# An LSTM step on one core of Trainium2: the output gate's products last, tanh of c transposed in place of h, and the bias copied into standing banks

## The chip, the core and the metric

The kernel runs on one core of a Trainium2 chip. Its engines are TensorE (PE, with its weight loads shown apart as PEld), VectorE (DVE), ScalarE (ACT), GpSimd (POOL) and SyncE (SP), which here only issues transfers. The metric is the device time of one execution in microseconds (us), less is better; the median over the runs is what is compared.

## The reference, cut to what matters

The program is a chain of two layers, each a graph layer and a feed-forward part. The second part of the first layer is an LSTM that runs over the first axis of the normalised input: 64 sequences are the batch and 256 positions are the steps, with 256 hidden units. Every step needs the h of the step before.

```python
def step(carry, xp):                       # xp: x @ W_ih.T + b_ih + b_hh
    h, c = carry
    gates = xp + h @ W_hh.T                # 64 x 1024
    i, f, g, o = jnp.split(gates, 4, axis=-1)
    c = jax.nn.sigmoid(f) * c + jax.nn.sigmoid(i) * jnp.tanh(g)
    h = jax.nn.sigmoid(o) * jnp.tanh(c)
    return ((h, c), h)
...
logits = jnp.einsum('bth,lh->btl', lstm_out, W_lin) + b_lin
g = jax.lax.stop_gradient(jnp.argmax(logits, axis=-1).astype(lstm_out.dtype))[..., None]
w = g * lstm_out
inc = jnp.cumsum(w, axis=1)
prefix = inc - w
suffix = inc[:, -1:, :] - inc
return 2.0 * lstm_out + prefix * fw_att + suffix * bw_att
```

## The kernel before, in words

The kernel goes through its stages one after the other: the first graph layer with its weights' preparation, the LSTM (lines 626 to 809), the second graph layer, and the second feed-forward part. The change is in the LSTM stage alone. All arithmetic there is in float32.

**Layout.** The 256 hidden units are split in two halves j of 128 units. A tile of 128 partitions holds half j=0 of the 64 sequences on partitions 0 to 63 and half j=1 on partitions 64 to 127, with 128 units along the free axis, so c, h and each gate are 128x128. The four gates of a step stand side by side in one bank of PSUM, 512 columns in the order i, f, g, o. The normalised input lies transposed in XT, and `hT` (128 units by 2 halves by 64 sequences) is h transposed: both serve as the 64-column weights of a product, while `w_ih` and `w_hh` stream past.

**A step's gates.** A bank is opened by one bfloat16 product (`open_gates`, L667) that writes the bias, given as three bfloat16 parts for each half. Then come four products with `w_ih` (`project`) and four with `w_hh`, all through `add_to_gates` (L673): K=2 parts of the contraction times two halves j, each half in its own 64 columns of the TensorE array (`tile_position`). The profile shows two rows of PE for each float32 product, so eight rows for each group of four. Banks come from a pool of four separate tiles; the bias is written three steps ahead and the input products run two steps ahead.

**The order of a step.** TensorE: the four `w_hh` products of step t, the four `w_ih` products of step t+2, the logits of step t-1 (L689, two products with a 256x2 weight), the bias row of step t+3, and the transpose of h (L798). `tc.issue_after` ties each of these behind the one before it; what remains of the order on every engine is the scheduler's. ScalarE: sigmoid of i and f (`sg`, L780), tanh of g (`gt`, L781), sigmoid of o (`so`, L789), tanh of c (`th`, L791). VectorE: f times c (L786), i times g (L787), their sum (L788), h = so times th (L795), and after TensorE's transpose into PSUM the copy to `hT` (L800).

**The sums.** Every four steps (TS) `summed` takes the four h of a buffer: VectorE adds b_lin and compares the two logits to a mask g on 64 partitions (L722, L723), a transfer copies g to the other 64 partitions (L726), and then VectorE forms w = h g, its running sums, and the result x1 + 2 h + prefix fb - w bw, which SP stores. It is a generator: a part of it is put behind the copy to `hT` of each following step.

Beside the LSTM's first steps, VectorE works on the parameters of the last stage (L812 to L1003), which need nothing of the LSTM; the scheduler places this work between the steps.

Of the kernel before, what the change touches and what calls it, by code (L numbers as in the profile page):

```python
# [143 lines left out]
def kernel(ctx: ExitStack, tc: tile.TileContext, a: dict, out: bass.AP):  # L144
# [482 lines left out]
    with (  # L627
# [7 lines left out]
        tc.tile_pool(name="ps_g2", bufs=4, space=PSUM) as ps_g,  # L635
        tc.tile_pool(name="ps_h2", bufs=1, space=PSUM) as ps_h,
        tc.tile_pool(name="ps_l2", bufs=2, space=PSUM) as ps_l,
# [4 lines left out]
        w_lin = wp.tile([P, K, 2], F32, name="w_lin")  # L642
        b_lin = wp.tile([B, 2], F32, name="b_lin")
        nc.sync.dma_start(w_ih, a["W_ihT"].rearrange("(k p) g -> p k g", p=P))
        nc.sync.dma_start(w_hh, a["W_hhT"].rearrange("(k p) g -> p k g", p=P))
        nc.sync.dma_start(w_lin, a["W_lin"])
        nc.sync.dma_start(b_lin, a["b_lin"].partition_broadcast(B))
# [16 lines left out]
        def open_gates(t):  # L664

            pg = ps_g.tile([P, 4 * P], F32, name=f"pg2_{t}", tag="pg2")
            return pg, nc.tensor.matmul(pg, halves, bias6, start=True, stop=False)  # L667

        def add_to_gates(pg, by, w, last):

            for k in range(K):
                for j in range(2):
                    ins = nc.tensor.matmul(  # L673
                        half(pg, j),
                        by(k),
                        gates_of(w, k, j),
                        start=False,
                        stop=(last and k == K - 1),
                        tile_position=(0, j * B),
                    )  # L680
            return ins

        def project(t, pg):

            return add_to_gates(pg, lambda k: XT[:, k, t, :], w_ih, t == 0)

        def logits(pl, t, hT):
            for k in range(K):
                nc.tensor.matmul(  # L689
                    pl[:, t % TS, :],  # L690
                    hT[:, k, :],
                    w_lin[:, k, :],
                    start=(k == 0),
                    stop=(k == K - 1),
                )
# [17 lines left out]
        def summed(t, h, pl):  # L713
# [4 lines left out]
            if t + 2 * TS < N:  # L718
                x1_of.append(x1_steps(t + 2 * TS))
            l0 = y2.tile([B, TS], F32, name=f"l0_{t}", tag="l0")  # L720
            g = y2.tile([P, TS], F32, name=f"g_{t}", tag="g")
            nc.vector.tensor_scalar(l0, pl[:, :, 0], b_lin[:, 0:1], None, ALU.add)  # L722
            nc.vector.scalar_tensor_tensor(  # L723
                g[:B, :], pl[:, :, 1], b_lin[:, 1:2], l0, ALU.add, ALU.is_gt
            )
            nc.sync.dma_start(g[B:, :], g[:B, :])  # L726
            nc.vector.scalar_tensor_tensor(x1, h, 2.0, x1, ALU.mult, ALU.add)
            yield
            w = q2.tile([P, TS, P], F32, name=f"w_{t}", tag="w")
            nc.vector.tensor_tensor(w, h, over_units(g), ALU.mult)  # L730
            yield
# [5 lines left out]
            for i in range(1, TS):  # L737
                nc.vector.tensor_tensor(pre[:, i, :], pre[:, i - 1, :], w[:, i - 1, :], ALU.add)
            total = y2.tile([P, P], F32, name=f"total_{t}", tag="total")
            nc.vector.tensor_tensor(total, pre[:, TS - 1, :], w[:, TS - 1, :], ALU.add)  # L740
            nc.vector.tensor_tensor(pre, pre, over_steps(fb), ALU.mult)
            yield
            nc.vector.tensor_tensor(w, w, over_steps(bw), ALU.mult)
            nc.vector.tensor_tensor(x1, x1, pre, ALU.add)
            nc.vector.tensor_tensor(x1, x1, w, ALU.subtract)
# [3 lines left out]
            yield  # L749

        ahead = [open_gates(t)[0] for t in range(3)]
        for t in range(2):
            last_ins = project(t, ahead[t])
        c_prev = hT = h_buf = total = None
        parts = iter(())
        x1_of = [x1_steps(0), x1_steps(TS)]
        for t in range(N):
            pg = ahead.pop(0)  # L760
            if t > 0:
                last_ins = add_to_gates(pg, lambda k: hT[:, k, :], w_hh, True)
            if t + 2 < N:
# [41 lines left out]
        for _ in summed(N - TS, h_buf, pl):  # L805
            pass
# [972 lines left out]
```

## Time and profile before

| what | before |
|---|---|
| median of 17 runs | 4962.22 us (4940.71 to 4976.26) |
| the profiled execution's own time | 4955.38 us |
| its span | 4953.6 us |
| busy: PE, DVE, ACT, POOL | 87%, 78%, 45%, 40% of the span |
| LSTM stage | 645 to 1930 us of the span |

A row of the profile is an instruction or a group of them: line and engine, the operation, what it writes and reads by the program's names, the shape, and times. In a timeline, the first two numbers are the start and the length in us, and the bracket at the end tells how long the engine had been idle and which instruction ended that. In a list of groups, the numbers after the bar are busy time in us and the mean of one in ns, then idle time ahead of them. Ends of TensorE's rows are modelled: rows overlap, so their lengths don't add up to time, and their starts tell the pace.

### The profile page before, as it was taken

To read this page: it belongs to the slowest core of one execution; us is meant where nothing else is said; L and a number is where in the kernel's file an instruction comes from. 1 tells how busy PE (TensorE), PEld (TensorE's weight loads), DVE (VectorE), ACT (ScalarE), POOL (GpSimd) and SP (SyncE) were. 2 spreads that over 40 slices of the span, in tenths; PEclk is the share of its full clock that TensorE was granted. 3 is DMA by queue.
4 is the path that set the end of the run, shared out by engine and by line. 5 is a ranking of instruction groups with operands and counts; after the bars stand their busy time and mean duration, and the time that the engine had idled before them with its cause. 6 is when DMAs were issued, how large, how long until landed. Compare 5 with 4: busy or idle time off the path is not lost. (4 is left out here: it accounts for less than half of the span.)

```text
span 4953.6 us, 59162 instructions
## 1 busy us (share of the span) xinstructions
PE 4300.8 (87%) x18365; PEld 2366.7 (48%) x18366; DVE 3867.3 (78%) x8648; ACT 2241.2 (45%) x4246; POOL 1994.2 (40%) x2505
## 2 busy tenths in 40 slices
PE   8999978999999996888882388989999998999998
PEld 5666633333333333666671144544455454444555
DVE  7888867555555555777788798998989998899994
ACT  3555521222222222555561255555655565555564
POOL 2222220000000002555550566666666666666661
PEclk9999989999999998999995689999999999999999
DMA  5222211211111113555541788888888888888892
GB/s 139 87 83 84 84 42 48 74 26 30 26 28 29 26 31 88 158 166 166 164 157 40 262 290 277 288 297 281 300 295 277 300 294 278 276 283 292 292 302 45
DMA packets 456279, 830.53 MB, mean 168 GB/s; under 512 B 51595, under 2 KB 309138, under 8 KB 455954
## 3 DMA queue, kind: packets, MB, share of 16 engines
q0 software_dynamic: 183184, 613.07, 37.3%
q1 hardware_dynamic: 270884, 210.42, 14.5%
q8 instruction: 148, 2.42, 0.2%
q10 hardware_dynamic: 1886, 3.16, 0.2%
q14 instruction: 177, 1.45, 0.1%
HBM read 700.45 MB, written 127.04 MB: 167 GB/s over the span
## 5 line engine op out<-in xcount | busy, mean ns | idle before, releaser
L1409 POOL DMA_INDIRECT row<-wT_d,num x1065 | 1052.2, 988 | 549.8 <-issue 253.5
L1433 DVE SCALAR_TENSOR_TENSOR top<-row,val,top 128x1024 f32<-128x1024 f32 x696 | 890.9, 1280 | 8.4 <-remote 3.5
L673 PE MATMUL pg<-w_hh,hT 128*64 128x512 f32 x2040 | 498.5, 610 | 91.5 <-DVE hT L800 91.0
L1521 PE MATMUL po<-w_d,fu 128*128 128x256 f32 x2048 | 564.6, 401 | 3.8 <-DVE fu L1502 2.4
L1441 PE MATMUL pc_cl<-xr,w_c 128*128 128x512 f32 x1024 | 506.8, 620 | 47.3 <-issue 39.1
L1441 PE MATMUL pc_gg<-xr,w_gt 128*128 128x512 f32 x1024 | 499.4, 612 | 33.0 <-ACT gg L1452 31.2
L1491 DVE SCALAR_TENSOR_TENSOR pv<-u,prm,pv 128x512 f32<-128x512 f32 x512 | 383.0, 748 | 173.4 <-PE pv L1478 99.2
L673 PE MATMUL pg<-w_ih,XT 128*64 128x512 f32 x2048 | 484.9, 595 | 2.9 <-issue 2.9
L1521 PEld LDWEIGHTS po<-w_d,fu 128*128 128x128 f32 x2048 | 376.0, 195 | 225.6 <-issue 182.5
L780 ACT ACTIVATE sg<-pg 128x256 f32<-128x256 f32 x256 | 98.1, 383 | 832.2 <-PE pg L673 826.0
L1054 POOL TENSOR_TENSOR adjT<-adjT,ident 128x128 f32<-128x128 f32 x128 | 60.9, 491 | 1009.2 <-DMA adjT<-in_adjT_dram 1008.9
L1484 ACT ACTIVATE u<-pa,prm 128x512 f32<-128x512 f32 x512 | 384.2, 777 | 168.7 <-remote 43.4
L1478 PE MATMUL pv<-cl,minus 128*128 128x512 f32 x512 | 278.7, 627 | 61.6 <-ACT pv L1473 44.0
L1452 ACT ACTIVATE gg<-pc_gg,prm 128x512 f32<-128x512 f32 x256 | 176.1, 689 | 315.9 <-PE pc_gg L1441 137.2
L1441 PEld LDWEIGHTS pc_cl<-xr,w_c 128*128 128x128 f32 x1024 | 196.8, 199 | 227.7 <-issue 208.5
L1441 PEld LDWEIGHTS pc_gg<-xr,w_gt 128*128 128x128 f32 x1024 | 193.0, 195 | 210.0 <-issue 165.1
L259 DVE TENSOR_SCALAR xn<-x,mv,rstd 128x256 f32<-128x256 f32 x512 | 200.9, 422 | 115.9 <-POOL rstd L252 110.7
L673 PEld LDWEIGHTS pg<-w_ih,XT 128*64 128x64 f32 x2048 | 148.2, 138 | 298.5 <-issue 298.5
L1534 POOL DMA_INDIRECT out_dram<-sum,perm x128 | 216.2, 1689 | 175.5 <-ACT sum L1531 123.8
L1452 ACT ACTIVATE cl<-pc_cl,prm 128x512 f32<-128x512 f32 x256 | 175.5, 688 | 244.8 <-PE pc_cl L1441 143.1
L786 DVE TENSOR_TENSOR cc<-sg,cc 128x128 f32<-128x128 f32 x255 | 74.5, 292 | 257.3 <-ACT sg L780 255.6
L673 PEld LDWEIGHTS pg<-w_hh,hT 128*64 128x64 f32 x2040 | 124.5, 137 | 288.5 <-issue 148.2
(407 smaller groups left out, 8324.2 us busy)
## 6 DMA issues: line engine op xcount, KB each, us to landing
adjT<-in_adjT_dram SPq DMA_DIRECT2D x128, 256.0 KB, 2.8
row<-wT_d,num POOLq DMA_INDIRECT x1065
x<-in_x_dram SPq DMA_DIRECT2D x64, 256.0 KB, 2.6
x_d<-x SPq DMA_DIRECT2D x64, 256.0 KB, 2.6
x1s<-x_d SPq DMA_DIRECT2D x128, 128.0 KB, 2.8
x_d<-x1s SPq DMA_DIRECT2D x128, 128.0 KB, 2.5
x<-x_d SPq DMA_DIRECT2D x64, 256.0 KB, 2.8
res_d<-x SPq DMA_DIRECT2D x64, 256.0 KB, 2.4
```

The source lines that it names most:

```text
L259: nc.vector.tensor_scalar(xn[:, c, :], x[:, c, :], mv[:, c, 0:1], rstd[:, c : c + 1], ALU.subtract, ALU.mult)
L673: ins = nc.tensor.matmul(half(pg, j), by(k), gates_of(w, k, j), start=False, stop=(last and k == K - 1), tile_position=(0, j * B),)
L780: nc.scalar.activation(sg, pg[:, : 2 * P], AF.Sigmoid)
L1409: return lambda: nc.gpsimd.indirect_dma_start(new(("row", g, q, r), [P, FF]), None, wT_d, bass.IndirectOffsetOnAxis(ap=tiles["num", g, q][ ...
L1433: nc.vector.scalar_tensor_tensor(now, tiles["row", g, q, r], v, was, ALU.add, ALU.max)
L1441: nc.tensor.matmul(pc, wgt[:, k, f * P : (f + 1) * P], tiles["xr", g][:, k, :], start=(k == 0), stop=(k == K - 1),)
L1452: nc.scalar.activation(new((n, g, f), [P, CH]), tiles["pc", g, n, f], AF.Gelu if n == "cl" else AF.Sigmoid, bias=ff.col["bc" if n == "cl" ...
L1478: return lambda: nc.tensor.matmul(tiles["pv", g, f], minus, tiles["cl", g, f], start=False, stop=True)
L1484: return lambda: nc.scalar.activation(new(("u", g, f, k), [P, CH]), tiles["pa", g, f], AF.Relu, bias=of, scale=sc)
L1491: nc.vector.scalar_tensor_tensor(pv, tiles["u", g, f, k], sg, pv, ALU.mult, ALU.add)
L1521: nc.tensor.matmul(tiles["po", g, h][:, c, :], tiles["fu", g, f][:, q * P : (q + 1) * P], ff.w_d[:, f, :], start=False, stop=last and c == ...
L1534: return lambda: nc.gpsimd.indirect_dma_start(out_rows, place(i, 1), tiles["sum", g, q // NC][:, q % NC, :], None, compute_op=ALU.add)
```

## The change

The four banks become one tile `gates` with four parts, made once. Each is opened once by the bias product before the loop; one of them is copied to `b_all` in SBUF, and in the loop ScalarE copies `b_all` into a bank again after its step has read it (L810 of the new file), so no bias product is left in the loop. The `w_hh` products are issued as four of 384 columns (i, f, g) and then four of 128 columns (o). Instead of h, TensorE transposes `so` (L798) and `th` (L805); ScalarE copies the first out of PSUM (`soT`), and VectorE multiplies it with the second straight into `hT` (L808); h itself is formed behind that. The four `w_ih` products of step t+2 are spread: two ahead of the transpose of `so`, one between the transposes, one behind. The logits are formed by GpSimd: h times each row of W_lin, added down to 16 columns, reduced by VectorE, and the two halves of units added by one product with a matrix `twin` for every four steps, which gives the mask on all 128 partitions and saves its transfer. GpSimd also multiplies w by bw. The weights of the logits are spread over partitions by six transfers ahead of the loop. The loop stands under `manual_schedule`: on TensorE, ScalarE and VectorE the loop's instructions keep the order of the program text.

```diff
--- before.py
+++ after.py
@@ -632,19 +632,28 @@
...
-        tc.tile_pool(name="ps_g2", bufs=4, space=PSUM) as ps_g,
+        tc.tile_pool(name="ps_g2", bufs=1, space=PSUM) as ps_g,
...
-        tc.tile_pool(name="ps_l2", bufs=2, space=PSUM) as ps_l,
+        tc.tile_pool(name="ps_l2", bufs=1, space=PSUM) as ps_l,
...
-        w_lin = wp.tile([P, K, 2], F32, name="w_lin")
-        b_lin = wp.tile([B, 2], F32, name="b_lin")
+        b_lin = wp.tile([P, 2], F32, name="b_lin")
         nc.sync.dma_start(w_ih, a["W_ihT"].rearrange("(k p) g -> p k g", p=P))
         nc.sync.dma_start(w_hh, a["W_hhT"].rearrange("(k p) g -> p k g", p=P))
-        nc.sync.dma_start(w_lin, a["W_lin"])
-        nc.sync.dma_start(b_lin, a["b_lin"].partition_broadcast(B))
+        nc.sync.dma_start(b_lin, a["b_lin"].partition_broadcast(P))
+        w_lin = wp.tile([P, 2, P], F32, name="w_lin")
+        lin_d = dram.tile([2, K, P], F32, name="lin_d")
+        for i in range(2):
+            nc.sync.dma_start(lin_d[i], a["W_lin"][:, :, i].rearrange("p k -> k p"))
+        for j in range(2):
+            for i in range(2):
+                nc.sync.dma_start(w_lin[j * B : (j + 1) * B, i, :], lin_d[i, j].partition_broadcast(B))
+        twin = wp.tile([P, P], F32, name="twin")
+        for j in range(2):
+            nc.vector.tensor_tensor(twin[:, j * B : (j + 1) * B], ident[:, :B], ident[:, B:], ALU.add)
...
@@ -661,38 +670,28 @@
...
-        def open_gates(t):
-            pg = ps_g.tile([P, 4 * P], F32, name=f"pg2_{t}", tag="pg2")
-            return pg, nc.tensor.matmul(pg, halves, bias6, start=True, stop=False)
-        def add_to_gates(pg, by, w, last):
+        AHEAD2 = 4
+        gates = ps_g.tile([P, AHEAD2, 4 * P], F32, name="gates")
+        b_all = wp.tile([P, 4 * P], F32, name="b_all")
+        def add_to_gates(t, by, w, which):
             for k in range(K):
                 for j in range(2):
-                    ins = nc.tensor.matmul(
-                        half(pg, j),
+                    nc.tensor.matmul(
+                        half(gates[:, t % AHEAD2, :], j)[:, which],
                         by(k),
-                        gates_of(w, k, j),
+                        gates_of(w, k, j)[:, which],
                         start=False,
-                        stop=(last and k == K - 1),
+                        stop=False,
                         tile_position=(0, j * B),
-                    )
-            return ins
-        def project(t, pg):
-            return add_to_gates(pg, lambda k: XT[:, k, t, :], w_ih, t == 0)
-        def logits(pl, t, hT):
-            for k in range(K):
-                nc.tensor.matmul(
-                    pl[:, t % TS, :],
-                    hT[:, k, :],
-                    w_lin[:, k, :],
-                    start=(k == 0),
-                    stop=(k == K - 1),
-                )
+                        skip_group_check=True,
+                    )
+                    yield
+        def project(t):
+            return add_to_gates(t, lambda k: XT[:, k, t, :], w_ih, slice(0, 4))
...
@@ -710,100 +709,116 @@
...
-        def summed(t, h, pl):
+        def summed(t, h):
...
-            l0 = y2.tile([B, TS], F32, name=f"l0_{t}", tag="l0")
-            g = y2.tile([P, TS], F32, name=f"g_{t}", tag="g")
-            nc.vector.tensor_scalar(l0, pl[:, :, 0], b_lin[:, 0:1], None, ALU.add)
-            nc.vector.scalar_tensor_tensor(
-                g[:B, :], pl[:, :, 1], b_lin[:, 1:2], l0, ALU.add, ALU.is_gt
-            )
-            nc.sync.dma_start(g[B:, :], g[:B, :])
+            lo = y2.tile([P, 2, TS], F32, name=f"lo_{t}", tag="lo")
+            few = q2.tile([P, 2, TS, 16], F32, name=f"few_{t}", tag="few")
+            for i in range(2):
+                hw = q2.tile([P, TS, P], F32, name=f"hw_{t}_{i}", tag="hw")
+                nc.gpsimd.tensor_tensor(hw, h, over_steps(w_lin[:, i, :]), ALU.mult)
+                for wide in (64, 32, 16):
+                    to = few[:, i] if wide == 16 else hw[:, :, :wide]
+                    nc.gpsimd.tensor_tensor(to, hw[:, :, :wide], hw[:, :, wide : 2 * wide], ALU.add)
             nc.vector.scalar_tensor_tensor(x1, h, 2.0, x1, ALU.mult, ALU.add)
             yield
+            yield
+            nc.vector.tensor_reduce(lo, few, AX.X, ALU.add)
+            pl = ps_l.tile([P, 2, TS], F32, name=f"pl_{t}", tag="pl")
+            nc.tensor.matmul(
+                pl.rearrange("p i t -> p (i t)"), twin, lo.rearrange("p i t -> p (i t)"), start=True, stop=True
+            )
+            l0 = y2.tile([P, TS], F32, name=f"l0_{t}", tag="l0")
+            g = y2.tile([P, TS], F32, name=f"g_{t}", tag="g")
+            nc.vector.tensor_scalar(l0, pl[:, 0, :], b_lin[:, 0:1], None, ALU.add)
+            nc.vector.scalar_tensor_tensor(g, pl[:, 1, :], b_lin[:, 1:2], l0, ALU.add, ALU.is_gt)
             w = q2.tile([P, TS, P], F32, name=f"w_{t}", tag="w")
             nc.vector.tensor_tensor(w, h, over_units(g), ALU.mult)
-            yield
             pre = q2.tile([P, TS, P], F32, name=f"pre_{t}", tag="pre")
...
-            for i in range(1, TS):
+            nc.vector.tensor_tensor(pre[:, 1, :], pre[:, 0, :], w[:, 0, :], ALU.add)
+            yield
+            for i in range(2, TS):
                 nc.vector.tensor_tensor(pre[:, i, :], pre[:, i - 1, :], w[:, i - 1, :], ALU.add)
             total = y2.tile([P, P], F32, name=f"total_{t}", tag="total")
             nc.vector.tensor_tensor(total, pre[:, TS - 1, :], w[:, TS - 1, :], ALU.add)
+            nc.gpsimd.tensor_tensor(w, w, over_steps(bw), ALU.mult)
             nc.vector.tensor_tensor(pre, pre, over_steps(fb), ALU.mult)
             yield
-            nc.vector.tensor_tensor(w, w, over_steps(bw), ALU.mult)
             nc.vector.tensor_tensor(x1, x1, pre, ALU.add)
+            yield
             nc.vector.tensor_tensor(x1, x1, w, ALU.subtract)
             for j in range(2):
                 nt, du = steps(t, j)
                 nc.sync.dma_start(x2_d[:, nt, du], x1[j * B : (j + 1) * B, :, :])
-            yield
-        ahead = [open_gates(t)[0] for t in range(3)]
+        for t in range(AHEAD2):
+            nc.tensor.matmul(gates[:, t, :], halves, bias6, start=True, stop=True)
+        nc.scalar.copy(b_all, gates[:, AHEAD2 - 1, :])
         for t in range(2):
-            last_ins = project(t, ahead[t])
+            for _ in project(t):
+                pass
         c_prev = hT = h_buf = total = None
-        parts = iter(())
+        parts = []
         x1_of = [x1_steps(0), x1_steps(TS)]
-        for t in range(N):
-            pg = ahead.pop(0)
-            if t > 0:
-                last_ins = add_to_gates(pg, lambda k: hT[:, k, :], w_hh, True)
-            if t + 2 < N:
-                with tc.issue_after(last_ins.ins):
-                    last_ins = project(t + 2, ahead[1])
-            if t > 0:
-                with tc.issue_after(last_ins.ins):
-                    if t % TS == 1:
-                        pl = ps_l.tile([B, TS, 2], F32, name=f"pl_{t}", tag="pl")
-                    logits(pl, t - 1, hT)
-                    if t % TS == 0:
-                        parts = summed(t - TS, h_buf, pl)
-            if t + 3 < N:
-                with tc.issue_after(last_ins.ins):
-                    pg_3, last_ins = open_gates(t + 3)
-                ahead.append(pg_3)
-            sg = p2.tile([P, 2 * P], F32, name=f"sg_{t}", tag="sg")
-            gt = p2.tile([P, P], F32, name=f"gt_{t}", tag="gt")
-            so = p2.tile([P, P], F32, name=f"so_{t}", tag="so")
-            nc.scalar.activation(sg, pg[:, : 2 * P], AF.Sigmoid)
-            nc.scalar.activation(gt, pg[:, 2 * P : 3 * P], AF.Tanh)
-            cc = p2.tile([P, P], F32, name=f"cc_{t}", tag="cc")
-            if t == 0:
-                nc.vector.tensor_tensor(cc, sg[:, :P], gt, ALU.mult)
-            else:
-                nc.vector.tensor_tensor(cc, sg[:, P:], c_prev, ALU.mult)
-                nc.vector.tensor_tensor(gt, sg[:, :P], gt, ALU.mult)
-                nc.vector.tensor_tensor(cc, cc, gt, ALU.add)
-            nc.scalar.activation(so, pg[:, 3 * P :], AF.Sigmoid)
-            th = p2.tile([P, P], F32, name=f"th_{t}", tag="th")
-            nc.scalar.activation(th, cc, AF.Tanh)
-            if t % TS == 0:
-                h_buf = p2.tile([P, TS, P], F32, name=f"h_{t}", tag="h")
-            h = h_buf[:, t % TS, :]
-            nc.vector.tensor_tensor(h, so, th, ALU.mult)
-            ph = ps_h.tile([P, K, B], F32, name=f"ph2_{t}", tag="ph2")
-            with tc.issue_after(last_ins.ins):
-                nc.tensor.transpose(ph.rearrange("p k b -> p (k b)"), h, ident)
-            hT = p2.tile([P, K, B], F32, name=f"hT_{t}", tag="hT")
-            copied = nc.vector.tensor_copy(hT, ph)
-            with tc.issue_after(copied.ins):
-                next(parts, None)
-            c_prev = cc
-        logits(pl, N - 1, hT)
-        for _ in summed(N - TS, h_buf, pl):
-            pass
+        ENG = mybir.EngineType
+        with tc.manual_schedule(engines={ENG.PE, ENG.Activation, ENG.DVE}):
+            for t in range(N):
+                pg = gates[:, t % AHEAD2, :]
+                if t > 0:
+                    for which in (slice(0, 3), slice(3, 4)):
+                        for _ in add_to_gates(t, lambda k: hT[:, k, :], w_hh, which):
+                            pass
+                later = project(t + 2) if t + 2 < N else iter(())
+                sg = p2.tile([P, 2 * P], F32, name=f"sg_{t}", tag="sg")
+                gt = p2.tile([P, P], F32, name=f"gt_{t}", tag="gt")
+                so = p2.tile([P, P], F32, name=f"so_{t}", tag="so")
+                cc = p2.tile([P, P], F32, name=f"cc_{t}", tag="cc")
+                nc.scalar.activation(sg, pg[:, : 2 * P], AF.Sigmoid)
+                nc.scalar.activation(gt, pg[:, 2 * P : 3 * P], AF.Tanh)
+                if t == 0:
+                    nc.vector.tensor_tensor(cc, sg[:, :P], gt, ALU.mult)
+                else:
+                    nc.vector.tensor_tensor(cc, sg[:, P:], c_prev, ALU.mult)
+                    nc.vector.tensor_tensor(gt, sg[:, :P], gt, ALU.mult)
+                    nc.vector.tensor_tensor(cc, cc, gt, ALU.add)
+                next(later, None)
+                next(later, None)
+                nc.scalar.activation(so, pg[:, 3 * P :], AF.Sigmoid)
+                pso = ps_h.tile([P, P], F32, name=f"pso_{t}", tag="pso")
+                nc.tensor.transpose(pso, so, ident)
+                next(later, None)
+                th = p2.tile([P, P], F32, name=f"th_{t}", tag="th")
+                nc.scalar.activation(th, cc, AF.Tanh)
+                soT = p2.tile([P, P], F32, name=f"soT_{t}", tag="soT")
+                nc.scalar.copy(soT, pso)
+                pth = ps_h.tile([P, P], F32, name=f"pth_{t}", tag="pth")
+                nc.tensor.transpose(pth, th, ident)
+                next(later, None)
+                hT = p2.tile([P, K, B], F32, name=f"hT_{t}", tag="hT")
+                nc.vector.tensor_tensor(hT.rearrange("p k b -> p (k b)"), pth, soT, ALU.mult)
+                if t + AHEAD2 < N:
+                    nc.scalar.copy(pg, b_all)
+                if t % TS == 0:
+                    h_was, h_buf = h_buf, p2.tile([P, TS, P], F32, name=f"h_{t}", tag="h")
+                    if t > 0:
+                        parts.append(summed(t - TS, h_was))
+                nc.vector.tensor_tensor(h_buf[:, t % TS, :], so, th, ALU.mult)
+                parts = [part for part in parts if next(part, part) is not part]
+                c_prev = cc
+        parts.append(summed(N - TS, h_buf))
+        for part in parts:
+            for _ in part:
+                pass
...
```

## The prediction

> **What bounds the kernel now.** I read the busy time by stage first, then the costliest groups, then the timeline of one step. The stretches view puts the LSTM at 645 to 1930 us, 1285 us of the 4953.6 us span. Its columns after the length are busy time of PE, PEld, DVE, ACT and POOL, the granted TensorE clock, DMA share and GB/s:
>
> ```profile
> 645.00:1930.00 1285.00, 1151.36 (x5686) 436.54 (x5686) 761.32 (x2482) 266.94 (x1028) 37.16 (x43) 0.99 0.15 37
> ```
>
> PE looks busy for 90% of it and POOL is nearly free. The timeline of one step tells what sets the pace (start, length, engine, line):
>
> ```profile
> 1506.19 1.94 PE L673 MATMUL pg<-w_hh,hT 128*64 128x512 f32 x8 [0.38 <-DVE hT L800]
> ...
> 1507.96 1.89 PE L673 MATMUL pg<-w_ih,XT 128*64 128x512 f32 x8
> ...
> 1508.24 0.38 ACT L780 ACTIVATE sg<-pg 128x256 f32<-128x256 f32 x1 [3.20 <-PE pg L673]
> ...
> 1508.52 0.27 ACT L781 ACTIVATE gt<-pg 128x128 f32<-128x128 f32 x1
> 1508.66 0.29 DVE L786 TENSOR_TENSOR cc<-sg,cc 128x128 f32<-128x128 f32 x1 [1.66 <-ACT sg L780]
> 1508.68 0.28 ACT L789 ACTIVATE so<-pg 128x128 f32<-128x128 f32 x1
> ...
> 1509.18 0.29 DVE L788 TENSOR_TENSOR cc<-cc,gt 128x128 f32<-128x128 f32 x1
> ...
> 1509.57 0.31 ACT L791 ACTIVATE th<-cc 128x128 f32<-128x128 f32 x1 [0.61 <-DVE cc L788]
> 1509.68 0.34 PE L689 MATMUL pl<-w_lin,hT 128*64 128x2 f32 x4
> ...
> 1509.95 0.39 PE L667 MATMUL pg<-bias,halves 6*128 6x512 bf16 x1
> ...
> 1510.35 0.30 PE L798 MATMUL ph<-ident,h 128*128 128x128 f32 x1
> 1510.69 0.29 DVE L800 COPY hT<-ph 128x128 f32<-128x128 f32 x1 [0.48 <-PE ph L798]
> ```
>
> This is one serial chain: products of w_hh, sigmoid, c, tanh, h, transpose, hT, and again. The next step's w_hh row starts at 1511.03, so a step is 4.84 us. The input products, logits and bias row (L673 on w_ih, L689, L667) fill the hole in PE between 1507.96 and 1510.34, and end just as h is ready (1509.91 + 0.29 = 1510.20): they hide. So only the chain counts, 254 times (from t=1 to t=255).
>
> **Units for the sum.** The eight w_hh rows start in pairs, one row for each column half j, 0.43 apart (the weight loads between them stand at 1506.68, 1507.11 and 1507.54), the first pair 0.05 late. A row lasts 0.59, so 0.16 past its 0.43. The stream goes with the columns: 0.32 for 384, 0.11 for 128. The gaps show the handovers: PE to ACT 0.11 (1508.13 to 1508.24), DVE to PE 0.05 (1510.98 to 1511.03), which I take for ACT to PE too.
>
> **What the change does to the chain.** Its meant gain: three gates' products end 0.43 earlier, and one DVE multiplication (0.29) falls out because hT is formed straight from the two transposed factors. But the built program, listed with the semaphores each instruction waits for, shows that all four gate banks are now one tile, and it is ordered as one thing, bank or no bank. In every step t of the new file:
>
> ```
> sg L786    waits for the last of step t's four output-gate products (L681)
> w_ih L681  (bank t+2), first product, waits for gt L787 (bank t)
> so L796    waits for the second w_ih product (bank t+2)
> copy L810  (bias into bank t) waits for the fourth w_ih product (bank t+2)
> w_hh L681  (bank t+1), next step, waits for the copy L810 (bank t), and for hT
> ```
>
> Before, each bank was a tile of its own and none of these waits but the first existed. So work that hid in the hole now stands in the chain. The order of three engines is fixed: behind so on ACT stands th, behind w_ih on PE stand both transposes. Walking the step from its first w_hh row at 0:
>
> 1. w_hh: 0.05 + 4 x 0.32 + 3 x 0.11 + the last row's 0.27 (0.11 + 0.16) = 1.93. sg at 2.04: nothing gained over the 2.05 of before, as it waits for the output gate all the same.
> 2. gt starts 0.28 after sg and lasts 0.27: 2.59. The first w_ih product: 2.64.
> 3. Two w_ih products, j=0 and j=1, run as pairs: 0.05 + 0.43 + 0.59, end 3.71. so at 3.82, end 4.10. c is long there (2.04 + 1.23 by the rows above = 3.27), but th is behind so, at about 4.00, end 4.31. Before, th began 1.33 after sg; now 1.96.
> 4. Transpose of so at 4.18 (0.05, and 0.03 from weight load to row). The third w_ih product follows 0.11 later and is alone, since a transpose stands between it and its partner: two rows of 0.43, one after the other. Transpose of th at 4.18 + 0.11 + 0.86 = 5.15.
> 5. Fourth w_ih product, alone too: 5.26, end 5.26 + 0.43 + 0.59 = 6.28.
> 6. The bias copy: 6.39. ACT's 128x512 copies out of PSUM mean 0.60, its SBUF to SBUF form 0.63 (below); SBUF to PSUM has no row. Both neighbours agree, so 0.60 (0.55 to 0.75): 6.99. Next w_hh: **7.04**. hT, ready at 5.45 + 0.04 + 0.29 = 5.78, no longer decides.
>
> ```profile
> L1062 ACT COPY xnT<-pt 128x512 f32<-128x512 f32 x64 | 36.0, 600 | 30.2 <-PE pt L272 30.2
> L560 ACT ACTIVATE e<-e 128x512 f32<-128x512 f32 x5 | 3.2, 630 | 5.8 <-DVE e L559 5.8
> ```
>
> Handovers with two semaphores cost up to 0.15 (h end 1510.20 to transpose 1510.35), and changing between 64-column products and transposes twice more a step may add 0 to 0.2: I take **7.1**, bounds 6.8 to 7.6. That is +2.26 a step, x 254 = +574 us (+498 to +701).
>
> **The edits beside the chain.** Removed bias row, logits and the g transfer: already hidden, worth 0; had PE been the bound they would have given 0.29 + 0.34 + 0.39. GpSimd's logits and w by bw: nine multiplications and additions in four steps, of 512, 256, 128 or 64 columns. 128x512 rows of GpSimd mean 1.29 to 1.48 us, 128x128 rows 0.49. So (2 x (1.48 + 0.8 + 0.49 + 0.4) + 1.48) = 7.8 us against 28 us of four steps, with the reduction that needs them two steps later: hidden. The new h multiplication, reduction, l0, g and pre on DVE stand behind hT (5.78) with no more than some 2.3 us, and DVE's next chain work is at 7.1 + 2.45: hidden, and 0.29 to 0.9 a step if that slack went. The small product of lo (L732) stands on PE ahead of the next w_hh and waits for DVE until about 6.6: inside the copy's shadow. Six more DMAs on SP and the bias copy at the start: once, 2 to 6 us. The step mean of before was 4.92, not 4.84 ((1923.2 - 672.6)/254): 22 us of the parameter work of L830 to L1003 on DVE delays early steps, and half of it or more now falls into slack: -10 to -22. These two nearly cancel; I take -6.
>
> Sum: 574 - 6 = +568 against the profiled execution's own 4955.38 us (span 4953.6). The median of the runs, 4962.22, is 6.8 above that, so **5530** on the scale of the median. What a measurement here can tell from no change is about 0.2%, 10 us.
>
> [...] In the listing, sg (columns 0 to 255) waits for output-gate products into columns 384 to 511 of the same bank; with separate tiles this wait would stay. [...]
>
> A longer step leaves PE more idle, so the clock is to be weighed. Granted clock before: 1.00 over 2427 to 2447 us with PE busy 14.26 of 20 us (0.71), 0.50 over 2621 to 2703 with 17.12 of 82 (0.21). My step has rows on PE for 1.93 + 1.07 + 2.10 of 7.1, 0.72, nearest the first: full clock. [...]
>
> **Rivals.**
> - *A lone product's two rows overlap.* If the pairs in the trace are a product's own two rows, steps 4 and 5 lose 0.43 each: 6.24, +1.40 x 254 - 6 = +350, 5312. For it: only pairs are seen in the trace. Against: two rows can hardly fill the same 64 columns of the array at once, and pairs fit the two halves j. 8%.
> - *The clock halves at times.* Half clock doubles the streams, 4.4 us a step. Reached in one step in seven: 254/7 x 4.4 = +160, 5690; in more, beyond. Against: the 0.71 row above. 6%.
> - *Faster: the waits bind nothing.* If what they wait for were done earlier than the waiter is ready otherwise, the chain would be w_hh 1.93, sg to th as now, transpose, hT: shorter than PE's own stream of 0.05 + 4 x 0.32 + 4 x 0.11 + 3 x 0.86 + 2 x 0.11 + the lo product, some 4.6 to 4.7, which would be the bound: -0.15 to -0.24 a step, 4900 to 4925. It decides if w_ih streams while sg and gt run, before gt ends. Against: the waits stand in every step from t=1 to t=251, and a bias copy that ends before hT is impossible while it waits for a product behind the transpose of th. 4%.
> - *The change does nothing* (the stage is bound elsewhere): DVE and POOL have slack, so nothing supports it. 1%.
>
> **How the numbers follow.** Forecast 5530 with its own range 5440 to 5660: 78%. The rivals: 8, 6, 4 and 1%; other mishaps 3%. The range reaches down to the lone-row case and up to the mild clock case: 5300 to 5690. Slower by over 0.2%: 95%; within: 1%; faster: 4%.
>
> **What would show it.** In the profile after: the LSTM from about 650 to some 2490 us, starts of w_hh 7.1 apart; sg 2.05 after w_hh as before; idle time of w_hh ended by ACT's copy (L810), not by hT; idle time of so ended by PE on w_ih; third and fourth w_ih products 0.86 long each with a transpose between; w_ih starting after gt. POOL at 25 to 30% there. A copy that ends before hT, or w_ih under sg, would refute it; a PEclk under 0.95 there would mean the clock case.

## The result and the profile after

The changed kernel takes 5638.98 us (median of 8 runs, 5632.04 to 5651.74), the kernel before 4959.38 us beside it: ratio 1.137, 95% interval 1.136 to 1.139, so **slower by 680 us**, where the prediction said 568. Direction and mechanism were right; the size was a sixth too small.

First the LSTM by stretch, same columns as in the prediction (the profiled span is 5644.1 us):

```profile
660.00:2610.00 1950.00, 1483.36 (x6832) 502.79 (x6830) 900.62 (x2470) 488.48 (x1537) 541.08 (x603) 0.98 0.09 25
```

PE's share fell from 90% to 76%: it waits now. For whom, the costliest groups say (busy time, mean ns of one | idle time just before, what ended it):

```profile
L681 PE MATMUL gates<-w_ih,XT 128*64 128x512 f32 x2048 | 830.0, 623 | 179.0 <-ACT gt L787 176.3
L681 PE MATMUL gates<-w_hh,hT 128*64 128x384 f32 x4080 | 507.4, 391 | 162.4 <-ACT gates L810 158.4
...
L810 ACT COPY gates<-b_all 128x512 f32<-128x512 f32 x252 | 148.5, 589 | 516.9 <-PE gates L681 516.9
```

The second line is the telling one (all four banks have one name here; that the product which ends ACT's idle time is the fourth of w_ih is told by the timeline below). The next step's w_hh is released by the bias copy of ACT, and the copy by a product of w_ih. Neither has anything to do with the next step's numbers: they share a tile. The timeline of one step (start, length, engine, line) shows the whole walk:

```profile
2003.72 1.95 PE L681 MATMUL gates<-w_hh,hT 128*64 128x384 f32 x16 [0.73 <-ACT gates L810]
...
2005.77 0.38 ACT L786 ACTIVATE sg<-gates 128x256 f32<-128x256 f32 x1 [2.11 <-PE gates L681]
...
2006.38 1.08 PE L681 MATMUL gates<-w_ih,XT 128*64 128x512 f32 x4 [0.71 <-ACT gt L787]
...
2007.50 0.28 ACT L796 ACTIVATE so<-gates 128x128 f32<-128x128 f32 x1 [1.18 <-PE gates L681]
...
2007.84 0.33 PE L798 MATMUL pso<-ident,so 128*128 128x128 f32 x1 [0.38 <-ACT so L796]
...
2008.09 1.07 PE L681 MATMUL gates<-w_ih,XT 128*64 128x512 f32 x2
...
2009.10 0.33 PE L805 MATMUL pth<-ident,th 128*128 128x128 f32 x1
...
2009.36 1.07 PE L681 MATMUL gates<-w_ih,XT 128*64 128x512 f32 x2
2009.53 0.29 DVE L808 TENSOR_TENSOR hT<-pth,soT 128x128 f32<-128x128 f32 x1 [2.52 <-PE pth L805]
...
2010.52 0.59 ACT L810 COPY gates<-b_all 128x512 f32<-128x512 f32 x1 [2.06 <-PE gates L681]
...
2011.16 0.54 PE L681 MATMUL gates<-w_hh,hT 128*64 128x384 f32 x2 [0.42 <-ACT gates L810]
```

hT ends at 2009.82, and the products that need it start at 2011.16. A step is 7.44 us. Two rows of w_ih alone (x2) last 1.07, as long as four in pairs (x4, 1.08).

The span grew by 690.5 us: 254 steps x 2.606 (7.443 against 4.837) = 662, and 4 more, the balance of +8 in the first 120 steps and -4 in the last ones, which have no bias copy to wait for; 14 before the first w_hh product (672.6 to 687.1); 10 behind the last.

### The profile page after: what moved, and what is told of

The parts are those of the page before. It is cut to its first block, busy times and chain, and to the rows that moved or that the text cites. A ratio compares the mean times of both kernels' runs of the same rounds, so it can differ in the third digit from the quotient of the medians.

```text
span 5644.1 us, 62850 instructions
## 1 busy us (share of the span) xinstructions
PE 4634.5 (82%) x19513; PEld 2430.1 (43%) x19514; DVE 4018.5 (71%) x8650; ACT 2462.2 (44%) x4755; POOL 2510.9 (44%) x3081
## 5 line engine op out<-in xcount | busy, mean ns | idle before, releaser
L681 PE MATMUL gates<-w_ih,XT 128*64 128x512 f32 x2048 | 830.0, 623 | 179.0 <-ACT gt L787 176.3
L723 POOL TENSOR_TENSOR hw<-h,w_lin 128x512 f32<-128x512 f32 x128 | 166.6, 1301 | 1290.9 <-DVE h L815 1286.2
L681 PE MATMUL gates<-w_hh,hT 128*64 128x384 f32 x4080 | 507.4, 391 | 162.4 <-ACT gates L810 158.4
L681 PEld LDWEIGHTS gates<-w_hh,hT 128*64 128x64 f32 x4080 | 257.5, 138 | 522.4 <-ACT gates L810 334.2
L808 DVE TENSOR_TENSOR hT<-pth,soT 128x128 f32<-128x128 f32 x256 | 74.4, 291 | 540.1 <-PE pth L805 540.1
L791 DVE TENSOR_TENSOR cc<-sg,cc 128x128 f32<-128x128 f32 x255 | 107.3, 421 | 406.9 <-ACT sg L786 406.7
L810 ACT COPY gates<-b_all 128x512 f32<-128x512 f32 x252 | 148.5, 589 | 516.9 <-PE gates L681 516.9
L786 ACT ACTIVATE sg<-gates 128x256 f32<-128x256 f32 x256 | 98.1, 383 | 561.1 <-PE gates L681 561.1
L681 PEld LDWEIGHTS gates<-w_ih,XT 128*64 128x64 f32 x2048 | 149.6, 135 | 308.0 <-ACT gt L787 239.1
```

The costliest lines, as they stand in the source:

```text
L681: nc.tensor.matmul(half(gates[:, t % AHEAD2, :], j)[:, which], by(k), gates_of(w, k, j)[:, which], start=False, stop=False, tile_position= ...
L723: nc.gpsimd.tensor_tensor(hw, h, over_steps(w_lin[:, i, :]), ALU.mult)
L810: nc.scalar.copy(pg, b_all)
```

## The experiments

The runs fell on chips of two speeds: the kernel before takes some 4775 us on one and 4967 on the other. The LSTM does not care (the kernel after: 1915.3 us from first to last w_hh product in its first profile, 1920.5 in a second one, on the fast chip); the stages behind it do (3041.7 and 2847.8 us). So times are told as the difference from the kernel before **on the same chip**, and steps are read from each trace. "Late" steps are those from the 121st on; the lengths of four late steps are medians, one for each place in the block of four steps that the sums take together. What the expectations call totals in us are on the scale of the slower chip.

**The kernel after once more**, no edit.

> The kernel after unchanged, on the chip of the run beside it: ratio 1.135 to 1.139, late steps 7.44 us, whichever chip it is; on a chip where the kernel before takes some 4775 us, about 1.143, since the stages behind the LSTM are shorter there and the LSTM is not.

5459.64 us, +684.7 over the kernel before (4774.97), ratio 1.143 (1.141 to 1.145), late steps 7.44. This is the reference for the next five.

**Four tiles.** Only the allocation changes:

```
-gates = ps_g.tile([P, AHEAD2, 4 * P], F32, name="gates")
+gates = [ps_g.tile([P, 4 * P], F32, name=f"gates_{t}") for t in range(AHEAD2)]
```

> The kernel after, but each of the four gate banks a tile of its own. Theory (the shared tile orders work that is independent): the waits of w_ih on gt, of so on w_ih, and of the next w_hh on the bias copy go, and what is left is PE's own stream: from the first w_hh row to the first w_ih product 1.77 us, a pair of w_ih products 0.86, turn of so and switch 0.3 to 0.5, third product alone 1.07, turn of th and switch 0.3, fourth product alone 1.0: a step of 5.2 to 5.4 us in place of 7.44. 254 steps x -2.1 = -545: about 5090 us (5060 to 5130), still slower than the kernel before by 2 to 3%. Rival (the added work itself is the cost: ACT's bias copy 0.59 and copy of soT 0.3, GpSimd slowing DVE): the step stays above 6.8 us, 5480 to 5640.

+249.0 (ratio 1.052, 1.050 to 1.055): **436 us gone with one tile made four**, and no instruction less. The rival falls. The same two groups now, PE's idle time before them almost nil:

```profile
L681 PE MATMUL gates<-w_ih,XT 128*64 128x512 f32 x2048 | 873.1, 610 | 2.7 <-DMA w_ih<-in_W_ihT_dram 2.7
L681 PE MATMUL gates<-w_hh,hT 128*64 128x384 f32 x4080 | 571.1, 393 | 0.4 <-DVE hT L808 0.4
```

But 545 was expected. Of every four late steps two last 4.81 and 5.13 us, as worked out or better; the other two 5.93 and 6.56. Something the theory did not have.

**Whole pairs.** One tile, third and fourth w_ih product together between the two transposes:

```
 nc.tensor.transpose(pso, so, ident)
 next(later, None)
+next(later, None)
...
 nc.tensor.transpose(pth, th, ident)
-next(later, None)
```

> The kernel after with its one tile, but the third and fourth w_ih products stand together, behind the transpose of so, and the transpose of th behind both. Theory (a lone product costs as much as a pair, about 1.07 us, since its two rows run one after the other): one lone product's 1.07 us goes and the switch of 0.26 with it, the copy starts at about 5.6 in place of 6.80 us: step 6.2 to 6.4, x 254: about 5345 us (5300 to 5390). Rival (both rows of a lone product would run as fast as a pair's, and the time between is the wait for th and c): step 7.2 to 7.45, 5580 to 5640.

+490.4 (1.103, 1.101 to 1.105), 194 under the kernel after; 294 was expected. Two of four steps last 6.25 and 6.26 us, in the range of the theory, the others 6.57 and 6.93. In the undisturbed ones the copy starts 5.54 us after w_hh in place of 6.80: the lone product did cost 1.26 us with its switch. The rival falls; the same two steps in four are too long again.

**No bias copy in the steps.** The gates of step 4 and later are added onto what the bank held, and with the values that result a loop behind the LSTM runs that the other runs' profiles do not show (DVE's L1701, 36925 us), 46552 us in all: only the LSTM's stretch is read.

```
-if t + AHEAD2 < N:
-    nc.scalar.copy(pg, b_all)
```

> The kernel after with its one tile, without the bias copy in the steps: the gates of steps 4 to 255 are added onto what the bank held, so the values are not the reference's. Theory (the copy stands in the chain behind the fourth w_ih product): the next w_hh then waits for PE itself, for the fourth product's rows, started 5.63 us after w_hh: step 6.45 to 6.55 in place of 7.44, x 254: about 5400 us (5370 to 5430). Rival (the copy lies beside other late work, hT or the block sums on DVE, that ends as late): step 7.2 or more, 5580 to 5640.

From first to last w_hh product 1741.3 us in place of 1920.5, late steps 6.69 in the mean (6.22, 6.54, 6.63, 7.34). The copy did stand in the chain, and it was worth 0.7 us a step in the mean, less than the 0.9 to 1.0 worked out, since two of four steps are again longer than the theory has it.

**Four tiles, all w_ih products first.** The two transposes then stand together:

```
-next(later, None)
-next(later, None)
+for _ in later:
+    pass
 nc.scalar.activation(so, pg[:, 3 * P :], AF.Sigmoid)
```

> The kernel after with four tiles, and all four w_ih products directly behind w_hh, then the transposes of so and th. Theory: no wait left in the chain but w_hh, c, th and PE's stream: w_ih ends about 3.66 us after the first w_hh row, the transposes stand at 3.7 to 3.9, hT ends about 4.4: step 4.45 to 4.6 us, below the 4.84 of the kernel before; 5639 - 254 x 2.9 = about 4900 us (4865 to 4930), 1.2% faster than before (0.6 to 2.0%). Rival (turning so and th apart and ACT's longer row of work eats the gain of the missing multiplication): step 4.8 to 5.0, 4950 to 5020, not faster than before.

+204.7 (1.043, 1.041 to 1.045), where less than zero was expected. **My theory was not complete.** Two of four steps last 4.61 us, at the upper end of what was worked out, and the other two 5.38 and 6.56. The timeline of a step of 6.56, DVE and POOL alone:

```profile
1717.36 1.77 POOL L752 TENSOR_TENSOR w<-w,bw 128x512 f32<-128x512 f32 x1 [0.23 <-DVE total L751]
1717.92 1.35 DVE L791 TENSOR_TENSOR cc<-sg,cc 128x128 f32<-128x128 f32 x1
1719.09 0.49 POOL L726 TENSOR_TENSOR hw<-hw 128x128 f32<-128x128 f32 x1
1719.20 0.54 DVE L792 TENSOR_TENSOR gt<-sg,gt 128x128 f32<-128x128 f32 x1
...
1720.06 1.29 POOL L723 TENSOR_TENSOR hw<-h,w_lin 128x512 f32<-128x512 f32 x1
...
1720.96 0.29 DVE L806 TENSOR_TENSOR hT<-pth,soT 128x128 f32<-128x128 f32 x1 [0.83 <-PE pth L804]
```

cc and gt take 0.29 and 0.28 in other steps. Here each ends some 0.15 us after the GpSimd operation under which it began (1717.36 + 1.77 = 1719.13, cc at 1719.27; 1719.58 and 1719.74). hT, which has one of its inputs in PSUM, is under a GpSimd operation too and keeps its 0.29. The kernel after has the same in its trace: cc (L791), with both inputs in SBUF, lasts up to 1.43 us, and hT (L808) never over 0.292 in 256 rows. The rows show that such a DVE operation lasts until the GpSimd operation has ended, not why. The prediction missed it.

The step of 5.38 has another cause. The small product of lo (L732) stands on PE ahead of the next w_hh, and waits there for DVE's reduction, which comes behind hT and h:

```profile
1709.03 0.29 DVE L806 TENSOR_TENSOR hT<-pth,soT 128x128 f32<-128x128 f32 x1 [1.03 <-ACT soT L802]
...
1709.43 0.28 DVE L730 TENSOR_REDUCE lo<-few 128x8 f32<-128x128 f32 x1
...
1709.86 0.36 PE L732 MATMUL pl<-lo,twin 128*128 128x8 f32 x2 [1.05 <-DVE lo L730]
...
1710.14 0.54 PE L681 MATMUL gates<-w_hh,hT 128*64 128x384 f32 x2
```

hT ends at 1709.32, and w_hh, which otherwise starts 0.05 behind it, starts at 1710.14: 0.77 late. The same product stands in front of w_hh in the runs above: the step with it lasts 5.93 and the step before it 5.13 in four tiles, 6.93 and 6.25 in whole pairs, 7.34 and 6.54 without the copy. And one place in four is not always 4.61: 14 of the 34 late steps behind a step of 6.56 last 6.29 (1742.8, for one), with the clock at half for 3.41 us in each.

The second theory: GpSimd's logits, not the block sums themselves, stretch two steps in four. Two runs tell it apart, one that takes GpSimd out, one that puts it alone into the kernel before.

**four_early with the logits on PE**, by the products of the kernel before, and w by bw on DVE:

```
 nc.tensor.transpose(pth, th, ident)
+if t > 0:
+    ...
+    logits(pl, t - 1, hT)
```

> four_early with the logits back on PE as in the kernel before (behind the transpose of th, of the step before) and w by bw on DVE, so that GpSimd does nothing for the LSTM. Theory (the two stretched steps in four are DVE waiting for GpSimd's two-input operations): all four phases 4.6 to 4.8 us, 30 to 70 us under the kernel before, ratio 0.985 to 0.996. Rival (the block sums themselves, in the fixed order of DVE behind h, delay c): two of four steps stay above 5.2 us, ratio 1.015 or more.

4908.53 against 4967.25: **58.7 us faster than the kernel before**, ratio 0.988 (0.985 to 0.990). All four late steps last 4.60 to 4.61. So the excess of four_early, 263 us, came with GpSimd's form of the logits: 244 in the LSTM's steps, 14 ahead of them, where its loads stand. GpSimd's operations against DVE's are not all of it: of the 3.4 us that four late steps lose, 2.0 are the step of 6.56, 0.8 the wait for the product of lo and 0.7, in the mean, the clock.

**The kernel before with GpSimd's logits alone**: loads of w_lin, twin and the function summed as in the kernel after, the step's chain as it was.

```
-if t % TS == 1:
-    pl = ps_l.tile([B, TS, 2], F32, ...)
-logits(pl, t - 1, hT)
-if t % TS == 0:
-    parts = summed(t - TS, h_buf, pl)
+if t > 0 and t % TS == 0:
+    parts.append(summed(t - TS, h_buf))
```

> The kernel before, with only the logits moved to GpSimd (its products, the w by bw multiplication, the sum over halves by a small product, the g transfer gone), the step's chain as it was. Theory from the trace of four_early, where a DVE operation with two SBUF inputs (cc, 128x128, 0.29 us) that starts under a GpSimd multiplication ends only 0.15 us after it and lasts 1.35 us: two of four steps are caught, +1.0 to 2.0 in one and +0.3 to 0.8 in the other: mean step 5.2 to 5.5 in place of 4.84, +90 to +170 us over the kernel before, ratio 1.02 to 1.035. Rival (the working of the prediction: 7.8 us of GpSimd hide in 19 us of four steps, DVE has slack): -15 to +20 us, ratio 0.997 to 1.004.

+402.2 (1.081, 1.078 to 1.084), more than twice the theory's most, and the rival, my prediction's "hidden: 0", is off by 400. Four successive steps, with granted clock as the third number from the end:

```profile
1716.89:1723.23 6.34, 5.58 (x20) 1.76 (x20) 3.03 (x12) 1.03 (x4) 0.68 (x1) 1.00 0.14 41
1723.23:1731.12 7.89, 4.42 (x18) 1.34 (x19) 6.68 (x10) 1.03 (x4) 6.62 (x9) 0.87 0.00 0
1731.12:1738.08 6.96, 6.58 (x19) 1.85 (x19) 2.57 (x8) 1.03 (x4) 0.00 (x0) 0.66 0.00 0
1738.08:1742.92 4.84, 4.27 (x19) 1.29 (x19) 1.97 (x7) 1.03 (x4) 0.00 (x0) 1.00 0.23 59
```

In the second step, the one with 6.62 us of POOL, the three chain operations last 1.38, 1.34 and 0.69 in place of 0.29 each, 2.5 us more, and the first starts 0.3 late, behind a block sum of DVE; with a slower transpose behind them, 3.0. Behind it PE has been idle for 3 us, the clock falls (0.87 in the mean of this step, 0.66 of the third), and the third step runs its w_hh rows 0.85 apart in place of 0.43: another 2.1 (1.3 in every other such step). The first loses 1.5: 0.8 since the small product of lo stands between the first w_hh pairs there, 0.4 since a w_ih row runs ahead of the last w_hh row, 0.2 for a block sum between two chain operations. Sum 6.2 in four steps, 1.56 a step, x 254 = 396. The theory had the stall; it had neither the clock nor the small product on PE.

**The kernel before with the two transposes alone**, h formed beside the chain (the pool of the logits' tile has one buffer in place of two):

```
-nc.vector.tensor_tensor(h, so, th, ALU.mult)
-nc.tensor.transpose(ph.rearrange("p k b -> p (k b)"), h, ident)
-copied = nc.vector.tensor_copy(hT, ph)
+tr = nc.tensor.transpose(pso, so, ident)
+nc.scalar.copy(soT, pso)
+nc.tensor.transpose(pth, th, ident)
+copied = nc.vector.tensor_tensor(hT.rearrange("p k b -> p (k b)"), pth, soT, ALU.mult)
+nc.vector.tensor_tensor(h, so, th, ALU.mult)
```

> The kernel before, with only tanh of c and the output gate turned in place of h, and hT formed from the two; banks, bias rows, logits and order of the other work as they were. Theory (the fill work w_ih, logits and bias row ends on PE at 4.15 us whether h is ready earlier or not, and the second transpose comes behind it): step 5.0 to 5.2 in place of 4.84, +40 to +90 us, ratio 1.008 to 1.02. Rival (one DVE multiplication of 0.29 falls out of the chain): step 4.55 to 4.65, -50 to -75 us, ratio 0.984 to 0.99.

+52.0 (1.011, 1.008 to 1.013), all late steps 5.08. One DVE multiplication fell out of the chain and the step got longer: th is ready at 3.69, but PE does w_ih, logits and bias until 4.08, and the two transposes come behind. So the first transpose starts only 0.08 earlier than that of h did (4.16). And hT now needs soT as well, so it waits for ACT's copy:

```profile
1705.02 0.33 PE L798 MATMUL pso<-ident,so 128*128 128x128 f32 x1
...
1705.38 0.27 ACT L800 COPY soT<-pso 128x128 f32<-128x128 f32 x1 [0.75 <-PE pso L798]
1705.68 0.29 DVE L804 TENSOR_TENSOR hT<-pth,soT 128x128 f32<-128x128 f32 x1 [1.46 <-ACT soT L800]
```

It starts 0.66 behind the first transpose, where the copy to hT of before started 0.34 behind its own: 0.32 - 0.08 = 0.24 longer. The gain that the edit was made of would need a PE that is free earlier.

**The kernel after with its logits on PE**, one tile and all waits kept; w by bw back on DVE, the old loads:

```
 nc.tensor.transpose(pth, th, ident)
 next(later, None)
+if t > 0:
+    ...
+    logits(pl, t - 1, hT)
```

> The kernel after, one tile and all its waits kept, but the logits back on PE (behind the fourth w_ih product, beside the bias copy) and w by bw on DVE, so that GpSimd does nothing for the LSTM and its six loads at the start are gone. Theory (in the step of 7.44 us GpSimd's work and the DVE operations it stretches hide behind the waits of the shared tile): late steps 7.40 to 7.48 us as in the kernel after; only the start (about 12 us before the first w_hh), the tail (about 8) and early steps gain: 15 to 45 us under the kernel after, ratio to the kernel before 1.128 to 1.134 where that of after is 1.137. Rival (GpSimd against DVE costs in the kernel after too): late steps 7.0 or less, 100 us or more under the kernel after, ratio 1.117 or less.

+646.4 (1.136, 1.134 to 1.138), 38 under the kernel after, late steps 7.44 still. So in the kernel after itself GpSimd is hidden, as predicted, behind the waits of the tile. What it costs there lies elsewhere: 12.7 us at the start, 24 in the first 120 steps, which also hold parameter work of DVE.

**Output gate in banks of its own**, on top of early_pe_logits: two banks for three gates, two for the output gate, input products one step ahead; the output gate's w_ih rows and the logits stand behind the transpose of th, while DVE forms hT.

```
-gates = [ps_g.tile([P, 4 * P], F32, name=f"gates_{t}") for t in range(AHEAD2)]
+AHEAD2 = 2
+ifg = [ps_g.tile([P, 3 * P], F32, name=f"ifg_{t}") for t in range(AHEAD2)]
+og = [ps_g.tile([P, P], F32, name=f"out_{t}") for t in range(AHEAD2)]
...
-later = project(t + 2) if t + 2 < N else iter(())
+later = project(t + 1) if t + 1 < N else iter(())
```

> early_pe_logits with the output gate in PSUM banks of its own (two banks for three gates, two for the output gate, input products one step ahead instead of two), so that sg need not wait for the output gate's products; the output gate's w_ih products and the logits stand behind the transpose of th. Theory (the wait of sg on the output gate is worth 0.44 us a step, as the chain decides): sg at 1.58 in place of 1.99, step 4.2 to 4.45 us, 100 to 160 us under the kernel before, ratio 0.967 to 0.98. Rival (PE's own stream is the bound then, and an earlier sg gives nothing): step 4.6 to 4.8, ratio 0.985 to 0.996.

4838.84, **128.4 us faster than the kernel before**, ratio 0.974 (0.971 to 0.978). Late steps 4.20. sg starts under the output gate's own products now:

```profile
1702.02 0.62 PE L673 MATMUL out<-w_hh,hT 128*64 128x128 f32 x8
...
1702.26 0.39 ACT L780 ACTIVATE sg<-ifg 128x256 f32<-128x256 f32 x1 [1.38 <-PE ifg L673]
```

The step began at 1700.68, so sg comes 1.58 after it, not 1.99 as in four_early. The rival, PE as the bound at 4.6, falls. This is the best kernel found. It keeps the change's ideas but for the shared tile, the places of the w_ih products and GpSimd's logits; what each of them gives by itself in it was not run.

## Why the prediction was right, and where it was not

Right, with the prediction's number first (from the first w_hh row): sg 2.04, measured 2.05; first w_ih 2.64, 2.66; pair end 3.71, 3.74; so 3.82, 3.78; transpose of so 4.18, 4.12. "The waits bind nothing" fell: each wait of the listing is in the profile as a releaser. "A lone product's two rows overlap" fell: 1.07 us for two rows. The clock stayed at 1.00 in the late steps (1580 to 2610 us), so that rival fell too. Four tiles showed by experiment, not only by the listing, that the shared tile is the cause: 436 of 685 us.

Terms that were mis-sized:

- *Steps 4 and 5, third and fourth w_ih product.* I let a transpose take 0.11 before the next product, by its columns alone. It takes 0.25 and 0.26: 0.165 is the distance of two transposes in a row (four_early: 3.595 to 3.760), and the rest, 0.09, comes with the change to 64-column products. And the third product took 1.01 until the transpose of th, not 0.86: the first row behind a transpose lasts 0.48, and 0.53 pass behind the second. Together 7.44 in place of 7.04 worked out and 7.1 taken. "Changing between 64-column products and transposes may add 0 to 0.2" was the right doubt; no row of before showed that range, and I took 0.06 of it. With the 7.44 and 4.84 unrounded, (2.606 - 2.26) x 254 = 88 us. The rows give some 0.09 to each change from transpose to product, and do not show what it is spent on.
- *Six more DMAs at the start, 2 to 6 us.* The first w_hh product came 14 us later. The runs show whose these are: with the new loads it stands at 686 to 693 us (seven profiles), without them at 673 to 678 (five).
- *Early steps, -10 to -22.* Measured +8 in the first 120 steps: they hold 29 us above the even pace of late steps, those of the kernel before 21. With the logits on PE they hold 10, so the half of the parameter work that was to fall into slack did, and GpSimd's form of the logits, "hidden: 0" in the sum, took it back and more: 34 in the second run of the kernel after. The last steps, without a bias copy, give -4. cc (L791) means 421 ns in the kernel after, where its rows in quiet steps last 290.
- *Behind the last step.* Not in the sum; 10 us, 4 of which go when the logits are on PE (after_pe_logits); the rest was not followed.

The last three make +28 (14 + 8 - 4 + 10) where I had -6. 88 + 34 = 122, and 568 + 122 = 690, the difference of the spans.

Right only under its condition: "GpSimd's logits: hidden". In this kernel they are (after_pe_logits: late steps equal to 0.01). The price that I named for lost cover, 0.29 to 0.9 us a step for DVE's own work, had the wrong cause: with the logits on PE, DVE's sums cost the chain nothing (4.60 to 4.61), and GpSimd's form of the logits cost 244 us in the steps of four_early (some 1.0 a step) and 1.6 a step in the kernel before, by the DVE operations that lasted longer under GpSimd's, the product of lo on PE and the clock. For the product of lo the prediction had said where it hides, "inside the copy's shadow", and there it does: 0.77 a time came to light when the shadow went. So that the time came out near was luck in this point: a worse wait covered a cost that I had put at nothing.

One reading of the timeline before was wrong, with little weight in the sum, where it is one of two reasons for 7.1 in place of 7.04: the 0.15 from the end of h (1510.20) to the transpose (1510.35) is no handover of two semaphores. PE's bias row lasts until 1510.34, so the hole in PE was full, and an earlier h could not have gained much, as the two transposes alone showed.

The wait of sg on the output gate's products was worth what split_pe_logits expected of it: with the output gate in a bank of its own the late step fell from 4.607 to 4.203, 0.40 where I had 0.44. In the stage it gave 71 us, not the 112 of 0.44 x 254, since the early steps are held by parameter work (4.80 to 4.66).

What stays open: why the gathers behind the LSTM run at 291 GB/s on one chip and 322 on the other; how much of the 24 us of early steps that after_pe_logits saves is DVE's wait for GpSimd and how much the clock, which is at half for 41 us of the LSTM in the second run of the kernel after and for 10 in after_pe_logits; and what makes the clock fall.

## What to carry to other kernels

Buffers that are used in turn should be separate tiles: one tile for four banks made work on one bank wait for work on another, and cost 436 us with not one instruction more. Work moved to an idle GpSimd is not free for DVE: in these runs a DVE operation of 0.29 us with two SBUF inputs that began under a GpSimd operation lasted until some 0.15 us behind its end, up to 1.43 us in all, so what counts is whether DVE's *chain* operations can meet it, not GpSimd's busy share. And what such work hands back to an engine that keeps its order, here one small product on PE, must not stand ahead of the chain's own instructions: it cost 0.77 us each time. An operation taken out of a serial chain is worth something only if what it waits for comes earlier as well: see what the next engine does at that moment.

## What the runs showed of the hardware

- A DVE operation of 0.29 us with two SBUF inputs that begins under a GpSimd operation ended some 0.15 us after it (1.35 us in all in four_early, up to 1.38 in before_pool_logits and 1.43 in the kernel after); with one input in PSUM it kept 0.29 (hT in the kernel after: at most 0.292 in 256 rows).
- TensorE's granted clock fell to half after short idle times of PE. In before_pool_logits the trace's clock record puts a halving at 1729.05, in the step with 0.87 in the mean: the last row had ended at 1727.20, 1.85 us before, and the whole idle stretch is 3.08 us. In whole_pairs it fell in seven late steps, which last 7.75 to 8.3 us; here behind a stretch of 3.41 us with PE busy for 2.09 and its longest idle time 0.94:

```profile
1669.39:1672.80 3.41, 2.09 (x12) 0.80 (x10) 0.69 (x3) 1.33 (x4) 0.00 (x0) 1.00 0.29 80
1672.80:1676.21 3.41, 3.41 (x17) 1.64 (x16) 1.56 (x5) 0.00 (x0) 0.00 (x0) 0.50 0.12 31
```

In the kernel after, with idle times of 0.71 and 0.73 in a step, it never fell in a late step (granted clock 1.00 from 1580 to 2610 us). What makes the clock fall is not shown.
- The same kernel, the one after, differs by 179 us between chips (medians 5638.98 and 5459.64). Its LSTM does not (1915.3 and 1920.5 us); the stages behind it took 3041.7 and 2847.8 us. A difference of kernels must come from one chip.
